# Layer 0 of a four-layer image network: images kept and stored in pairs, one plane kept by halves, one sum moved

## Chip, cores and metric

The kernel runs on one core of one Trainium2 chip. The metric is the device time of one execution in microseconds (us), and the time before is the median of three runs. The core has five engines that run side by side, each taking its instructions strictly in order: PE (TensorE, matrix products), DVE (VectorE), ACT (ScalarE), POOL (GpSimd) and SP (SyncE), which in this kernel issues the transfers between main memory and the on-chip memory.

## What is computed

Four layers, each of the form `x = x + layer(group_norm(x))`, on 32 images of 96 channels and 56 x 56 pixels. The change lies in layer 0, an inverted bottleneck with a gate:

```python
def _L0_conv_ref(x, ...):
    identity = x
    h = jnp.einsum('nchw,oc->nohw', x, w_exp)            # 96 -> 576 channels
    h = jax.nn.silu(_bn(h, g1, b1, m1, v1))
    h = jax.lax.conv_general_dilated(h, w_dw, ...)       # 3x3, each channel by itself
    h = jax.nn.silu(_bn(h, g2, b2, m2, v2))
    s = h.mean(axis=(2, 3))
    s = jax.nn.silu(s @ w_se1.T + b_se1)
    s = jax.nn.sigmoid(s @ w_se2.T + b_se2)
    h = h * s[:, :, None, None]
    h = jnp.einsum('nchw,oc->nohw', h, w_proj)           # 576 -> 96
    h = _bn(h, g3, b3, m3, v3)
    return h + identity

def _gn(v, G=32, eps=1e-5):      # mean and variance over 3 channels x 56 x 56 of one image
...
x = x + _L0_conv_ref(_gn(x), ...)
```

Layer 1 is a wavelet convolution, layer 2 a quantised bottleneck, layer 3 a 9 x 9 convolution of each channel by itself. Between the layers the images lie in main memory as `y`, in which one row of 14 pixels of all 32 images is 32 x 14 x 4 = 1792 bytes: one image has 56 bytes of each such row, a pair of neighbours has 112.

## The kernel before

Layer 0 takes one image after the other, as 96 partitions (channels) by 3136 pixels. The pixels are stored by phase: every fourth column of a tile of 14 rows lies together, so a tile is 4 x 14 rows of 14 pixels. The 576 middle channels are five blocks of 128 partitions: blocks 0 to 2 whole, block 3 whole but convolved in two halves, block 4 with its 64 channels held twice.

One image passes these steps, which the order string `L0_ORDER` (line 59) names by letters. `s` sums the pixels on ACT (`sums`, line 267), `u` sums over the three channels of a group with a small matrix product on PE (`group_sum`), `m` makes the mean on DVE; `q`, `v`, `w` do the same for the squared deviation, and the reciprocal root `rstd` is made on POOL (line 282). `n` normalises on ACT (`xn`, line 295), `r` adds the residual's factor in place (line 301). `eki` expands block k for row tile i on PE (line 309) and puts SiLU of it into a padded plane on ACT (line 313). Blocks 0 to 2 are convolved by nine taps: `f` is the first, on ACT (line 321), `t` one of the other eight, on DVE (line 326). Blocks 3 and 4 are convolved on PE with diagonal matrices (`a`, `c`, line 349), and ACT takes the results out (line 332). `g0` to `g4` make the gate and the gated projection weights `wg`, `p` projects on PE (lines 407 to 410), `d` adds to the image on DVE (line 415), `o` stores it.

The order within one engine is exactly that of the string; a letter followed by `-` belongs to the image before, by `+` to the next one. So the loop is a pipeline over three images, and an engine that waits at a letter also holds back everything that stands behind it on this engine. Three banks of PSUM, the memory that PE writes, are shared by expansion, convolution and projection.

`store` (line 420 and on) issues six transfers of image b, 196 KB each (line 425), then `fetch(b + 3)` (line 196) into the buffer of that image, one of three, and then an equal share of the transfers named `aside`, which lay out convolution matrices of later layers in main memory (lines 520 and 547). `fetch` can be issued only when the image's six stores have landed, and it stands in SP's queue among the others.

Ahead of the loop, `tables()` makes filters for the layers 1 and 3: DVE fills the wavelet tables `zt`, POOL makes the diffusion filter (lines 1108 to 1132), SP stores them. These parts are placed by a scheduler; some buffers of the loop lie where the tables were and wait for their stores.

Of the kernel before, what the change touches and what calls it, by code (L numbers as in the profile page):

```python
# [33 lines left out]
PITCH = W + 1  # L34
NPAD = (H + 2) * PITCH + 2
PAIRS = C // 2
# [25 lines left out]
L0_ORDER = """  # L62
    e00 e01 e02 e03 z0- f0 a3- z2- c1- e10 e11 t01 t02 g0- e12 t03 e30 e40 g1- s+ e13 t04 g2- g3-
    e31 e32 t05 e33 g4- t06 t07 u+ f1 m+ t11 p0- p1- q+ t08 d0- v+ w+ p2- t12 e41 d1- p3- d2- t13
    t14 e20 e21 d3- o- b+ t15 e42 t16 e43 e22 e23 f2 a0 t17 t21 a1 n+ t22 t18 t23 t24 t25 t26 t27 r
# [60 lines left out]

def padded(pool, nc, n, dtype, name):

    out = []
    for i in range(n):  # L130
        t = pool.tile([128, NPAD], dtype, tag=f"{name}{i}", name=f"{name}{i}")
        nc.gpsimd.memset(t[:, : PITCH + 1], 0.0)
        nc.gpsimd.memset(t[:, PITCH : PITCH * (H + 2) : PITCH], 0.0)
        nc.gpsimd.memset(t[:, PITCH * (H + 1) :], 0.0)
        out.append(t)
    return out
# [14 lines left out]


def tiles(t):

    return t.rearrange("c (t p r) q -> c t p (r q)", t=NP, p=NPH)

# [7 lines left out]
@with_exitstack  # L164
def layer0(ctx, tc, S, x, w, y0, norm1, tables, aside):


# [22 lines left out]

    xs = {}

    def fetch(b):
        if b < B:
            xs[b] = pool.tile([C, H * NPH, W4], F32, tag="xt", name="xt", bufs=3)
            nc.sync.dma_start(xs[b], x[b])

# [9 lines left out]
    out4 = load("l0_out", [C, 4])  # L207
    fetch(1)
    fetch(2)

# [20 lines left out]

    eye2 = cp.tile([128, HALF], F32, tag="eye2", name="eye2")
    diag = cp.tile([128, 2, 9, HALF], F32, tag="diag", name="diag")
    hpad = padded(cp, nc, 4, F32, "hpad")
    mv_all = cp.tile([C, B, 2], F32, tag="mv0", name="mv0")
    h2s = [cp.tile([128, H, W], F32, tag=f"h2{i}", name=f"h2{i}") for i in range(2)]


    tables()
    nc.vector.tensor_tensor(eye2, S.ident[:, :HALF], S.ident[:, HALF:], ALU.add)  # L240
# [3 lines left out]
    late = ctx.enter_context(tc.tile_pool(name="l0l", bufs=1))  # L244
    h2s += [late.tile([128, H, W], F32, tag=f"h2{i}", name=f"h2{i}") for i in (2, 3)]
    hab = late.tile([128, NP, 2, NT], F32, tag="hab", name="hab")
    wg = late.tile([128, ND + 1, C], F32, tag="wg", name="wg")
    h2s.append(late.tile([128, H, W], F32, tag="h24", name="h24"))
    hc = late.tile([128, 2, 2, NT], F32, tag="hc", name="hc")

    ims = {}

    def image(b):

        if b not in ims:
            ims[b] = {
                "b": b, "xt": xs.pop(b), "h2": [None] * DV, "ps": [None] * NP,
                "pad": [hpad[(DV * b + k) % 2] for k in range(DV)] + hpad[2:],
                "ss": sm.tile([128, ND], F32, tag="ss", name="ss"),
            }  # L260
        return ims[b]


    def sums(im, name, func, bias):
        im[name] = sm.tile([C, 1], F32, tag=name, name=name)
        junk = pool.tile([C, HW], BF16, tag="junk", name="junk", bufs=1)
        nc.scalar.activation(junk, im["xt"].rearrange("c r q -> c (r q)"), func, bias=bias,
                             accum_out=im[name])

    def group_sum(im, name):  # L270
        im["ps" + name] = psm.tile([C, 1], F32, tag="sm", name="pn")
        nc.tensor.matmul(im["ps" + name], S.grp, im[name], start=True, stop=True)

    def mean(im):
        im["nm"] = sm.tile([C, 1], F32, tag="nm", name="nm")
        nc.vector.tensor_scalar(im["nm"], im["pss1"], -1.0 / HW, None, ALU.mult)

    def deviation(im):
        ve = sm.tile([C, 1], F32, tag="ve", name="ve")
        nc.vector.tensor_scalar(ve, im["pss2"], 1.0 / HW, EPS_GN, ALU.mult, ALU.add)  # L280
        im["rstd"] = sm.tile([C, 1], F32, tag="rstd", name="rstd")
        nc.gpsimd.tensor_tensor(im["rstd"], ve, S.mhalf[:C, :1], ALU.pow)
# [9 lines left out]
    def normalise(im):  # L292
        im["xn"] = pool.tile([C, 2, H, W2], F32, tag="xn", name="xn", bufs=1)
        for p in range(NPH):
            nc.scalar.activation(
                im["xn"][:, p % 2].rearrange("c (t r) (q m) -> c m t (r q)", t=NP, m=2)[:, p // 2],
                tiles(im["xt"])[:, :, p], AF.Identity, bias=im["nb"], scale=im["rstd"])
# [5 lines left out]
    def expand(im, k, i):  # L303

        c = COL[k]
        rows = slice(2 * i * RT, 2 * (i + 1) * RT)
        ps = psum.tile([128, 2, 512], F32, tag="mm", name="ps")
        for j in range(2):
            nc.tensor.matmul(  # L309
                ps[:, j, :NT], wexp[:, k * 128 : k * 128 + 128],  # L310
                im["xn"][:, j, rows, :].rearrange("c h w -> c (h w)"), start=True, stop=True,
            )
        nc.scalar.activation(  # L313
            window(im["pad"][k], 128, 0, 0, 2 * i * RT, 2 * RT).rearrange("p r (w j) -> p j r w", j=2),
            ps[:, :, :NT].rearrange("p j (r w) -> p j r w", w=W2),
            AF.Silu, bias=bi[0][:, c : c + 1], scale=sc[0][:, c : c + 1],
        )

# [16 lines left out]
    def end_block(im, k):  # L335
        silu2(k, im["h2"][k], im["h2"][k], im["ss"][:, k : k + 1])

    def quarters(k, pad, tiles):


        ps = psum.tile([128, 2, 512], F32, tag="mm", name="psd")
        for t in range(9):
            for j in range(2):
                for r in range(2):
                    c = r ^ j
                    p = slice(r * HALF, (r + 1) * HALF)
                    at = (2 * tiles[r] * RT + t // 3) * PITCH + t % 3
                    v = pad[p, at : at + 2 * RT * PITCH].rearrange("p (r w) -> p r w", w=PITCH)
                    nc.tensor.matmul(  # L349
                        ps[c * HALF : (c + 1) * HALF, j, :NT].rearrange("p (r w) -> p r w", w=W2),  # L350
                        diag[p, k - AB, t, :], v[:, :, j:W:2], start=(t == 0), stop=(t == 8),
                    )
        return ps
# [9 lines left out]
    def depthwise_c(im, i):  # L363

        if i == 0:
            im["hc"] = hc
            im["pc"] = sm.tile([128, 2], F32, tag="pc", name="pc")
        ps = quarters(CC, im["pad"][CC], (2 * i, 2 * i + 1))
        silu2(5, im["hc"][:, i], ps[:, :, :NT], im["pc"][:, i : i + 1])
# [30 lines left out]
    def project(im, i):  # L400
        wg = im["wg"]
        rows = slice(2 * i * RT, 2 * (i + 1) * RT)
        ps = im["ps"][i] = psum.tile([128, 2, 512], F32, tag="mm", name="psj")
        for j in range(2):
            out = ps[:C, j, :NT]
            for k in range(DV):
                nc.tensor.matmul(out.rearrange("c (r w) -> c r w", w=W2), wg[:, k, :],  # L407
                                 im["h2"][k][:, rows, j::2], start=(k == 0), stop=False)
            nc.tensor.matmul(out, wg[:, 3 + j, :], im["hab"][:, i, j, :], start=False, stop=False)  # L409
            nc.tensor.matmul(out, wg[:, 5 + (i % 2 ^ j), :], im["hc"][:, i // 2, j, :], start=False, stop=True)  # L410

    def add(im, i):
        for j in range(2):
            v = tiles(im["xt"])[:, i, j::2]
            nc.vector.scalar_tensor_tensor(
                v, im["ps"][i][:C, j, :NT].rearrange("c (x m) -> c m x", m=2), sc3, v, ALU.mult, ALU.add)
        if im["b"] == B - 1:
            store_tile(nc, y0, im, i)

    def store(im):  # L420
        b, xt = im["b"], im["xt"]
        channel_stats(nc, sm, xt, mv_all[:, b, :], "t")
        if b < B - 1:
            for to, of in groups(xt, y0, lambda y: y[:, :, b, :], store=True):
                nc.sync.dma_start(to, of)  # L425
        fetch(b + 3)
        if b < B - 4:
# [452 lines left out]
def layer2(ctx, tc, S, k2, y1, y2, norm3):  # L880
# [187 lines left out]
    def store(im):  # L1068
        b = im["b"]
        channel_stats(nc, sm, im["xt"], mv_all[:, b, :], "t")  # L1070
        if b == B - 2:
            for to, of in groups(im["xt"], y2, lambda y: y[:, :, b, :], store=True):
                nc.sync.dma_start(to, of)
        elif b % 2 and b < B - 1:
            for to, of in groups(im["pair"], y2, lambda y: y[:, :, b - 1 : b + 1, :], store=True):
                nc.sync.dma_start(to, of)
            fetch(b + 5)
# [291 lines left out]
```

## Time and profile before

| | |
|---|---|
| median of 3 runs | 6499.85 us (6497.44 to 6500.72) |
| profiled execution | 6501.16 us |
| its span, first to last instruction | 6499.3 us |
| mean granted TensorE clock | 0.964 of full speed |
| PE busy in the span | 6025.5 us (93%) |
| DVE busy | 5168.3 us (80%) |
| ACT busy | 3953.6 us (61%) |
| POOL busy | 234.1 us (4%) |
| layer 0's last addition | at 3339.9 us |

Times inside the profile are counted from the first instruction. A busy share is a mean over stages with different limits, so what matters for a change in layer 0 is read from the first half of the trace: the waits, the order of time on each engine, and the same stretch of the loop in different images. A matrix product of 32-bit numbers is two instructions in the trace.

### The profile page before, as it was taken

What the parts mean: (1) busy time and instruction counts of PE and PEld (TensorE: products, weight loads), DVE (VectorE), ACT (ScalarE), POOL (GpSimd) and SP (SyncE); (2) the same over time, 40 slices, a digit from 0 to 9 for tenths busy, and PEclk for the clock granted to TensorE, in tenths of its full rate; (3) what the DMA queues carried; (4) which work ended last, traced back from release to release, by engine and by line L of the source; (5) the groups of instructions that cost most, each with busy time, mean ns of one, the idle gap of its engine ahead of it and who ended that gap; (6) DMA issues with size and microseconds to landing.
All of it is one profiled execution on the core that took longest, in us unless ns stands there. A gap on an engine that the chain in (4) does not pass through costs nothing.

```text
span 6499.3 us, 115397 instructions
## 1 busy us (share of the span) xinstructions
PE 6025.5 (93%) x49064; PEld 3599.1 (55%) x49064; DVE 5168.3 (80%) x5469; ACT 3953.6 (61%) x5268; POOL 234.1 (4%) x157
## 2 busy tenths in 40 slices
PE   6989989998998998989969999989999999999699
PEld 3444444444444444444535666667777777778344
DVE  8989979898998998989957766657777767676587
ACT  6556555655656565556635565557767766677355
POOL 4000000000000000000000000000000000000000
PEclk8999999999999999989979999999999999999899
DMA  2486475839539439474655776656869695953888
GB/s 80 29 41 50 41 43 41 46 44 40 47 41 41 43 47 42 39 41 39 17 60 143 141 155 150 143 36 45 48 42 50 44 49 41 51 38 31 166 253 248
DMA packets 1631554, 452.94 MB, mean 70 GB/s; under 512 B 1447406, under 2 KB 1625318, under 8 KB 1627582
## 3 DMA queue, kind: packets, MB, share of 16 engines
q1 hardware_dynamic: 1631038, 445.55, 65.7%
q8 instruction: 386, 6.32, 0.6%
q14 instruction: 130, 1.06, 0.1%
HBM read 284.44 MB, written 214.08 MB: 77 GB/s over the span
## 4 chain that ended last, share of the span: by engine, by line
PE 71%; ACT 9%; DMA 9%; SPq 6%; DVE 3%; issue 1%; POOL 1%; ACTq 0%; DVEq 0%
PE psd L349 14%; PE psd L1019 11%; PE ps L309 9%; PE psj L407 8%; PE pc L735 6%; PE ps L1000 5%; SPq L425 4%; DMA y<-xt 4%; PE pc L1175 3%; PE psj L1056 3%; PE psj L409 3%; PE psj L410 2%; ACT hi L972 2%; ACT a L990 2%; DVE h L326 2%; PE pc L719 2%
## 5 line engine op out<-in xcount | busy, mean ns | idle before, releaser
L326 DVE SCALAR_TENSOR_TENSOR h<-hpad,l_wdw,h 128x3136 f32<-128x3136 f32 x768 | 2659.6, 3480 | 28.7 <-ACT h L321 14.9
L349 PE MATMUL psd<-hpad,diag 64*64 64x392 f32 x13824 | 1239.6, 512 | 13.4 <-issue 13.4
L313 ACT ACTIVATE hpad<-ps,o,s 128x784 f32<-128x784 f32 x640 | 684.3, 1081 | 773.3 <-PE ps L309 771.3
L309 PE MATMUL ps<-xn,l_wexp 96*128 96x392 f32 x2560 | 931.6, 516 | 135.6 <-ACT hpad L313 129.1
L1019 PE MATMUL psd<-apad,diag 64*64 64x392 bf16 x20736 | 931.5, 332 | 110.4 <-ACT a L990 57.2
L349 PEld LDWEIGHTS psd<-hpad,diag 64*64 64x64 f32 x13824 | 547.5, 132 | 694.9 <-issue 656.8
L1019 PEld LDWEIGHTS <-diag 64*64 64x64 bf16 x20736 | 695.6, 107 | 342.3 <-issue 164.7
L309 PEld LDWEIGHTS ps<-xn,l_wexp 96*128 96x128 f32 x2560 | 493.4, 197 | 524.2 <-ACT hpad L313 135.3
L565 ACT COPY T<-raw 32x112 f32<-32x112 f32 (+2 forms) x1440 | 462.8, 384 | 308.1 <-DMA raw<-tdiff 223.3
L990 ACT ACTIVATE u<-ps,o,s 128x784 int16<-128x784 f32 x576 | 536.3, 1002 | 162.0 <-PE ps L1000 143.6
L990 ACT ACTIVATE a<-psd,o,s 128x784 int16<-128x784 f32 x448 | 423.7, 999 | 327.7 <-PE psd L1019 327.7
L407 PE MATMUL psj<-h,wg 128*96 128x392 f32 x1536 | 591.4, 520 | 27.9 <-ACT hpad L313 26.4
L1000 PE MATMUL ps<-hi,l_w1q 96*128 96x392 f32 x1280 | 462.4, 361 | 10.0 <-ACT hi L972 9.2
L1175 PE MATMUL pc<-x,T 128*112 128x416 f32 (+1 forms) x1152 | 415.2, 523 | 48.1 <-DMA raw<-tdiff 47.6
L735 PE MATMUL pc<-x,T 128*112 128x416 f32 (+1 forms) x1152 | 445.8, 523 | 0.0
L1000 PE MATMUL ps<-lo,l_w1q 96*128 96x392 f32 x1280 | 438.0, 342 | 0.0
L407 PEld LDWEIGHTS psj<-h,wg 128*96 128x96 f32 x1536 | 249.4, 166 | 289.3 <-issue 258.3
L1175 PEld LDWEIGHTS pc<-x,T 128*112 128x112 f32 x1152 | 204.7, 178 | 258.1 <-issue 240.7
L332 ACT ACTIVATE hab<-psd,o,s 128x392 f32<-128x392 f32 x256 | 170.6, 671 | 263.5 <-PE psd L349 263.5
L332 ACT ACTIVATE h<-h,o,s 128x3136 f32<-128x3136 f32 x96 | 287.9, 2999 | 19.7 <-DVE h L326 19.7
L321 ACT ACTIVATE h<-hpad,l_wdw 128x3136 f32<-128x3136 f32 x96 | 279.1, 2907 | 9.3 <-DMA twav<-zwav 8.3
L735 PEld LDWEIGHTS pc<-x,T 128*112 128x112 f32 x1152 | 190.9, 178 | 143.9 <-issue 143.9
(202 smaller groups left out, 6793.5 us busy)
## 6 DMA issues: line engine op xcount, KB each, us to landing
X<-y SPq DMA_DIRECT2D x192, 392.0 KB
xt<-in_x_dram SPq DMA_DIRECT2D x32, 1176.0 KB
y<-xt SPq DMA_DIRECT2D x192, 196.0 KB
y<-y SPq DMA_DIRECT2D x96, 392.0 KB
xt<-y SPq DMA_DIRECT2D x96, 392.0 KB
out_dram<-y SPq DMA_DIRECT2D x96, 392.0 KB
y<-xt SPq DMA_DIRECT2D x90, 392.0 KB
twav<-zwav SPq DMA_DIRECT2D x768, 36.8 KB
```

The source lines that it names most:

```text
L309: nc.tensor.matmul(ps[:, j, :NT], wexp[:, k * 128 : k * 128 + 128], im["xn"][:, j, rows, :].rearrange("c h w -> c (h w)"), start=True, sto ...
L313: nc.scalar.activation(window(im["pad"][k], 128, 0, 0, 2 * i * RT, 2 * RT).rearrange("p r (w j) -> p j r w", j=2), ps[:, :, :NT].rearrange ...
L326: nc.vector.scalar_tensor_tensor(h2, window(im["pad"][k], 128, t // 3 - 1, t % 3 - 1, 0, H), wdw[:, k, t : t + 1], h2, ALU.mult, ALU.add,)
L332: nc.scalar.activation(view, ps, AF.Silu, bias=bi[1][:, c : c + 1], scale=sc[1][:, c : c + 1], accum_out=accum)
L349: nc.tensor.matmul(ps[c * HALF : (c + 1) * HALF, j, :NT].rearrange("p (r w) -> p r w", w=W2), diag[p, k - AB, t, :], v[:, :, j:W:2], start ...
L407: nc.tensor.matmul(out.rearrange("c (r w) -> c r w", w=W2), wg[:, k, :], im["h2"][k][:, rows, j::2], start=(k == 0), stop=False)
L565: nc.scalar.copy(to.rearrange("x t (p s) -> x t p s", p=NPH), v[:, k])
L735: nc.tensor.matmul(ps[:PH, to], st["T"][j][:, h, k, :], st["x"][:, j, h, of], start=False, stop=(n == NK - 1))
L990: nc.scalar.activation(out, ps, AF.Identity, bias=o[:, c : c + 1], scale=s[:, c : c + 1])
L1000: nc.tensor.matmul(ps[:, j, :NT], w1[:, k * 128 : k * 128 + 128], im[part][:, r0 : r0 + RT, :].rearrange("c h w -> c (h w)"), start=(part ...
L1019: nc.tensor.matmul(ps[q, j, :NT].rearrange("p (r w) -> p r w", w=W), diag[p, k, t, :], v, start=(t == 0), stop=(t == 8))
L1175: nc.tensor.matmul(ps[:, :, to], st["T"][:, h, k, :], st["x"][:, h, :, of], start=(n == 0), stop=(n == NK - 1))
```

## The change

- An input transfer brings two images, laid out side by side row by row, into one of two pair buffers; the second buffer lies in the pool that comes after the tables. The result of two images is stored together, at the odd one: six transfers of 392 KB, by the function that layer 2 used already. The last two images are stored as before.
- Block 4's plane no longer holds all 56 rows twice: partitions 0 to 63 hold the upper 28 rows, 64 to 127 the lower 28, each with one further row from the other half. Two of its four expansions per image get a second, small ACT instruction for that row.
- The matrix products of convolution and projection read columns as neighbouring pairs instead of every second one, and the projection writes PSUM so that each phase lies together. The addition then reads PSUM in order.
- Each of the two pixel sums is taken in four tiles with four partial sums; the group product has four columns, and a DVE reduction (`total`) stands ahead of the mean and of the deviation.
- In the order, `s+` moves from before `e13` to behind `t07`, ahead of `f1`; `u+` and `m+` move behind `p0-`.
- The unit matrix `eye2` lies in `wg` now, so the diagonal matrices are made after the tables' buffers are free.

```diff
-    e00 e01 e02 e03 z0- f0 a3- z2- c1- e10 e11 t01 t02 g0- e12 t03 e30 e40 g1- s+ e13 t04 g2- g3-
-    e31 e32 t05 e33 g4- t06 t07 u+ f1 m+ t11 p0- p1- q+ t08 d0- v+ w+ p2- t12 e41 d1- p3- d2- t13
+    e00 e01 e02 e03 z0- f0 a3- z2- c1- e10 e11 t01 t02 g0- e12 t03 e30 e40 g1- e13 t04 g2- g3-
+    e31 e32 t05 e33 g4- t06 t07 s+ f1 t11 p0- u+ m+ p1- q+ t08 d0- v+ w+ p2- t12 e41 d1- p3- d2- t13
...
+def store_images(nc, y, im):
+
+    b = im["b"]
+    if b == B - 2:
+        t, at = im["xt"], b
+    elif b % 2 and b < B - 1:
+        t, at = im["pair"], slice(b - 1, b + 1)
+    else:
+        return
+    for to, of in groups(t, y, lambda y: y[:, :, at, :], store=True):
+        nc.sync.dma_start(to, of)
...
+    pairs = [cp.tile([C, H * NPH, 2, W4], F32, tag="xt0", name="xt0")]
 
     def fetch(b):
+
         if b < B:
-            xs[b] = pool.tile([C, H * NPH, W4], F32, tag="xt", name="xt", bufs=3)
-            nc.sync.dma_start(xs[b], x[b])
+            pair = pairs[b // 2 % 2]
+            nc.sync.dma_start(pair, x[b // 2])
+            for j in range(2):
+                xs[b + j] = pair, pair[:, :, j, :]
...
-    fetch(1)
-    fetch(2)
...
-    hpad = padded(cp, nc, 4, F32, "hpad")
+    hpad = padded(cp, nc, 3, F32, "hpad") + padded(cp, nc, 1, F32, "hhalf", HH)
...
     tables()
+    late = ctx.enter_context(tc.tile_pool(name="l0l", bufs=1))
...
+    wg = late.tile([128, ND + 1, C], F32, tag="wg", name="wg")
+    eye2 = wg[:, 0, :HALF]
     nc.vector.tensor_tensor(eye2, S.ident[:, :HALF], S.ident[:, HALF:], ALU.add)
...
+    pairs.append(late.tile([C, H * NPH, 2, W4], F32, tag="xt1", name="xt1"))
+    fetch(2)
...
     def sums(im, name, func, bias):
-        im[name] = sm.tile([C, 1], F32, tag=name, name=name)
-        junk = pool.tile([C, HW], BF16, tag="junk", name="junk", bufs=1)
-        nc.scalar.activation(junk, im["xt"].rearrange("c r q -> c (r q)"), func, bias=bias,
-                             accum_out=im[name])
+
+        im[name] = sm.tile([C, NP], F32, tag=name, name=name)
+        for i in range(NP):
+            junk = pool.tile([C, 2 * RT * NPH, W4], BF16, tag="junk", name="junk", bufs=1)
+            nc.scalar.activation(junk, im["xt"][:, i * 2 * RT * NPH : (i + 1) * 2 * RT * NPH], func, bias=bias,
+                                 accum_out=im[name][:, i : i + 1])
...
+    def total(im, name):
+        t = sm.tile([C, 1], F32, tag=f"t{name}", name=f"t{name}")
+        nc.vector.tensor_reduce(t, im["ps" + name], AX.X, ALU.add)
+        return t
...
+        parts = [(slice(128), 2 * i * RT, slice(2 * RT))]
+        if k == CC:
+            lo, up = slice(64), slice(64, 128)
+            parts = [(up if i // 2 else lo, i % 2 * 2 * RT, slice(2 * RT))]
+            parts += [[], [(up, -1, slice(2 * RT - 1, 2 * RT))], [(lo, HH, slice(1))], []][i]
...
+    def phases(v, j):
+
+        return v.rearrange("p r (q j m) -> p j r q m", j=2, m=2)[:, j]
...
-                        diag[p, k - AB, t, :], v[:, :, j:W:2], start=(t == 0), stop=(t == 8),
+                        diag[p, k - AB, t, :], phases(v[:, :, :W], j), start=(t == 0), stop=(t == 8),
...
-            out = ps[:C, j, :NT]
+            out = ps[:C, j, :NT].rearrange("c (m r q) -> c r q m", m=2, q=W4)
...
-                nc.tensor.matmul(out.rearrange("c (r w) -> c r w", w=W2), wg[:, k, :],
-                                 im["h2"][k][:, rows, j::2], start=(k == 0), stop=False)
+                nc.tensor.matmul(out, wg[:, k, :], phases(im["h2"][k][:, rows], j), start=(k == 0), stop=False)
...
-        fetch(b + 3)
+        store_images(nc, y0, im)
+        if b % 2:
+            fetch(b + 3)
```

More of the change, by code (lines that the diff above doesn't have):

```diff
@@ L34 @@
 PITCH = W + 1
-NPAD = (H + 2) * PITCH + 2
 PAIRS = C // 2
@@ L124, in run_steps, with padded @@
                 step[s[0]](image(b), *map(int, s.rstrip("+-")[1:]))
-def padded(pool, nc, n, dtype, name):
+def padded(pool, nc, n, dtype, name, rows=H):
     out = []
     for i in range(n):
-        t = pool.tile([128, NPAD], dtype, tag=f"{name}{i}", name=f"{name}{i}")
+        t = pool.tile([128, (rows + 2) * PITCH + 2], dtype, tag=f"{name}{i}", name=f"{name}{i}")
         nc.gpsimd.memset(t[:, : PITCH + 1], 0.0)
-        nc.gpsimd.memset(t[:, PITCH : PITCH * (H + 2) : PITCH], 0.0)
-        nc.gpsimd.memset(t[:, PITCH * (H + 1) :], 0.0)
+        nc.gpsimd.memset(t[:, PITCH : PITCH * (rows + 2) : PITCH], 0.0)
+        nc.gpsimd.memset(t[:, PITCH * (rows + 1) :], 0.0)
         out.append(t)
@@ L150, in store_tile @@
         nc.sync.dma_start(to, of)
+def store_images(nc, y, im):
[8 more added lines that the diff above has]
+        nc.sync.dma_start(to, of)
 def tiles(t):
-    return t.rearrange("c (t p r) q -> c t p (r q)", t=NP, p=NPH)
+    return t.rearrange("c (t p r) q -> c t p r q", t=NP, p=NPH)
 def window(t, p, dy, dx, r0, rows):
@@ L230, in layer0 @@
     nc.vector.tensor_tensor(bi3, out4[:, 1:2], bi3, ALU.subtract)
-    eye2 = cp.tile([128, HALF], F32, tag="eye2", name="eye2")
     diag = cp.tile([128, 2, 9, HALF], F32, tag="diag", name="diag")
-    hpad = padded(cp, nc, 4, F32, "hpad")
+    hpad = padded(cp, nc, 3, F32, "hpad") + padded(cp, nc, 1, F32, "hhalf", HH)
     mv_all = cp.tile([C, B, 2], F32, tag="mv0", name="mv0")
@@ L239, in layer0 @@
     tables()
+    late = ctx.enter_context(tc.tile_pool(name="l0l", bufs=1))
+    h2s += [late.tile([128, H, W], F32, tag=f"h2{i}", name=f"h2{i}") for i in (2, 3)]
+    hab = late.tile([128, NP, 2, NT], F32, tag="hab", name="hab")
+    wg = late.tile([128, ND + 1, C], F32, tag="wg", name="wg")
+    eye2 = wg[:, 0, :HALF]
     nc.vector.tensor_tensor(eye2, S.ident[:, :HALF], S.ident[:, HALF:], ALU.add)
@@ L243, in layer0 @@
             nc.vector.tensor_scalar(diag[:, k - AB, t, :], eye2, wdw[:, COL[k], t : t + 1], None, ALU.mult)
[L244 to L247, printed above, removed]
     h2s.append(late.tile([128, H, W], F32, tag="h24", name="h24"))
     hc = late.tile([128, 2, 2, NT], F32, tag="hc", name="hc")
+    pairs.append(late.tile([C, H * NPH, 2, W4], F32, tag="xt1", name="xt1"))
+    fetch(2)
     ims = {}
@@ L255, in image @@
         if b not in ims:
+            pair, xt = xs.pop(b)
             ims[b] = {
-                "b": b, "xt": xs.pop(b), "h2": [None] * DV, "ps": [None] * NP,
+                "b": b, "pair": pair, "xt": xt, "h2": [None] * DV, "ps": [None] * NP,
                 "pad": [hpad[(DV * b + k) % 2] for k in range(DV)] + hpad[2:],
@@ L264, in sums @@
     def sums(im, name, func, bias):
-        im[name] = sm.tile([C, 1], F32, tag=name, name=name)
-        junk = pool.tile([C, HW], BF16, tag="junk", name="junk", bufs=1)
-        nc.scalar.activation(junk, im["xt"].rearrange("c r q -> c (r q)"), func, bias=bias,
-                             accum_out=im[name])
-    def group_sum(im, name):
-        im["ps" + name] = psm.tile([C, 1], F32, tag="sm", name="pn")
-        nc.tensor.matmul(im["ps" + name], S.grp, im[name], start=True, stop=True)
+        im[name] = sm.tile([C, NP], F32, tag=name, name=name)
[3 more added lines that the diff above has]
+                                 accum_out=im[name][:, i : i + 1])
+    def group_sum(im, name):
+        ps = psm.tile([C, NP], F32, tag="sm", name="pn")
+        nc.tensor.matmul(ps, S.grp, im[name], start=True, stop=True)
+        im["ps" + name] = ps
+    def total(im, name):
+        t = sm.tile([C, 1], F32, tag=f"t{name}", name=f"t{name}")
+        nc.vector.tensor_reduce(t, im["ps" + name], AX.X, ALU.add)
+        return t
     def mean(im):
         im["nm"] = sm.tile([C, 1], F32, tag="nm", name="nm")
-        nc.vector.tensor_scalar(im["nm"], im["pss1"], -1.0 / HW, None, ALU.mult)
+        nc.vector.tensor_scalar(im["nm"], total(im, "s1"), -1.0 / HW, None, ALU.mult)
     def deviation(im):
         ve = sm.tile([C, 1], F32, tag="ve", name="ve")
-        nc.vector.tensor_scalar(ve, im["pss2"], 1.0 / HW, EPS_GN, ALU.mult, ALU.add)
+        nc.vector.tensor_scalar(ve, total(im, "s2"), 1.0 / HW, EPS_GN, ALU.mult, ALU.add)
         im["rstd"] = sm.tile([C, 1], F32, tag="rstd", name="rstd")
@@ L295, in normalise @@
             nc.scalar.activation(
-                im["xn"][:, p % 2].rearrange("c (t r) (q m) -> c m t (r q)", t=NP, m=2)[:, p // 2],
+                im["xn"][:, p % 2].rearrange("c (t r) (q m) -> c m t r q", t=NP, m=2)[:, p // 2],
                 tiles(im["xt"])[:, :, p], AF.Identity, bias=im["nb"], scale=im["rstd"])
@@ L312, in expand @@
             )
[L313 to L317, printed above, removed]
+        parts = [(slice(128), 2 * i * RT, slice(2 * RT))]
[3 more added lines that the diff above has]
+            parts += [[], [(up, -1, slice(2 * RT - 1, 2 * RT))], [(lo, HH, slice(1))], []][i]
+        for p, r0, rows in parts:
+            n = rows.stop - (rows.start or 0)
+            nc.scalar.activation(
+                window(im["pad"][k][p], p.stop - (p.start or 0), 0, 0, r0, n).rearrange("p r (w j) -> p j r w", j=2),
+                ps[p, :, :NT].rearrange("p j (r w) -> p j r w", w=W2)[:, :, rows],
+                AF.Silu, bias=bi[0][p, c : c + 1], scale=sc[0][p, c : c + 1],
+            )
     def first_tap(im, k):
@@ L349, in quarters @@
                     nc.tensor.matmul(
-                        ps[c * HALF : (c + 1) * HALF, j, :NT].rearrange("p (r w) -> p r w", w=W2),
-                        diag[p, k - AB, t, :], v[:, :, j:W:2], start=(t == 0), stop=(t == 8),
+                        ps[c * HALF : (c + 1) * HALF, j, :NT].rearrange("p (r q m) -> p r q m", q=W4, m=2),
+                        diag[p, k - AB, t, :], phases(v[:, :, :W], j), start=(t == 0), stop=(t == 8),
                     )
@@ L367, in depthwise_c @@
             im["pc"] = sm.tile([128, 2], F32, tag="pc", name="pc")
-        ps = quarters(CC, im["pad"][CC], (2 * i, 2 * i + 1))
+        ps = quarters(CC, im["pad"][CC], (i, i))
         silu2(5, im["hc"][:, i], ps[:, :, :NT], im["pc"][:, i : i + 1])
@@ L404, in project @@
         for j in range(2):
-            out = ps[:C, j, :NT]
+            out = ps[:C, j, :NT].rearrange("c (m r q) -> c r q m", m=2, q=W4)
+            hab, hc = (im[n].rearrange("p i j (r q m) -> p i j r q m", q=W4, m=2) for n in ("hab", "hc"))
             for k in range(DV):
-                nc.tensor.matmul(out.rearrange("c (r w) -> c r w", w=W2), wg[:, k, :],
-                                 im["h2"][k][:, rows, j::2], start=(k == 0), stop=False)
-            nc.tensor.matmul(out, wg[:, 3 + j, :], im["hab"][:, i, j, :], start=False, stop=False)
-            nc.tensor.matmul(out, wg[:, 5 + (i % 2 ^ j), :], im["hc"][:, i // 2, j, :], start=False, stop=True)
+                nc.tensor.matmul(out, wg[:, k, :], phases(im["h2"][k][:, rows], j), start=(k == 0), stop=False)
+            nc.tensor.matmul(out, wg[:, 3 + j, :], hab[:, i, j], start=False, stop=False)
+            nc.tensor.matmul(out, wg[:, 5 + (i // 2 ^ j), :], hc[:, i % 2, j], start=False, stop=True)
     def add(im, i):
         for j in range(2):
-            v = tiles(im["xt"])[:, i, j::2]
+            n = 2 * i + j
+            v = im["xt"][:, 2 * n * 2 * RT : 2 * (n + 1) * 2 * RT, :]
             nc.vector.scalar_tensor_tensor(
-                v, im["ps"][i][:C, j, :NT].rearrange("c (x m) -> c m x", m=2), sc3, v, ALU.mult, ALU.add)
+                v, im["ps"][i][:C, j, :NT].rearrange("c (r q) -> c r q", q=W4), sc3, v, ALU.mult, ALU.add)
         if im["b"] == B - 1:
@@ L420, in store @@
     def store(im):
[L421 to L425, printed above, removed]
-        fetch(b + 3)
+        b = im["b"]
+        channel_stats(nc, sm, im["xt"], mv_all[:, b, :], "t")
+        store_images(nc, y0, im)
+        if b % 2:
+            fetch(b + 3)
         if b < B - 4:
@@ L1070, in store @@
         channel_stats(nc, sm, im["xt"], mv_all[:, b, :], "t")
[L1071 to L1076, printed above, removed]
+        store_images(nc, y2, im)
+        if b % 2:
             fetch(b + 5)
@@ L1354 @@
     nc = _bacc.Bacc("TRN2", target_bir_lowering=False, num_devices=1)
-    x = a["x"].reshape(B, C, NP, 2 * RT, W4, NPH).transpose(0, 1, 2, 5, 3, 4).reshape(B, C, H * NPH, W4)
+    x = a["x"].reshape(B // 2, 2, C, NP, 2 * RT, W4, NPH).transpose(0, 2, 3, 6, 4, 1, 5).reshape(B // 2, C, H * NPH, 2, W4)
     arrays = {"x": np.ascontiguousarray(x), **layouts(a)}
```

## The prediction

> **What bounds the kernel now.** First the waits, over layer 0's loop (who waited for whom, us in total, times, longest):
>
> ```profile
> ACT junk L267 <- DMA xt<-in_x_dram: 138.6, 7, 27.0
> PE ps L309 <- ACT hpad L313: 127.0, 7, 26.0
> ```
>
> Seven times the first sum waits for its image, and PE behind it waits nearly as long, for ACT to empty PSUM. SP's timeline says why (start, duration): a late image, a normal one, and a pair store of layer 2.
>
> ```profile
> 1518.64 53.45 SPq L425 DMA_DIRECT2D y<-xt  x6
> 1592.60 0.32 SPq L196 DMA_DIRECT2D xt<-in_x_dram  x1
> ...
> 1832.76 27.23 SPq L425 DMA_DIRECT2D y<-xt  x6
> 1870.77 0.34 SPq L196 DMA_DIRECT2D xt<-in_x_dram  x1
> ...
> 4408.93 32.10 SPq L1076 DMA_DIRECT2D y<-xt  x6
> ```
>
> Where six stores take over 50 us instead of 27 to 31, the fetch comes at 74 us instead of 38. Windows from store to store give the price (length; PE, PEld, DVE, ACT, POOL busy; clock; DMA):
>
> ```profile
> 1518.64:1639.97 121.33, 98.67 (x622) 48.76 (x621) 92.78 (x52) 62.14 (x62) 3.63 (x1) 0.89 1.33 36
> 1832.76:1929.07 96.31, 94.90 (x622) 47.28 (x621) 92.69 (x52) 62.00 (x62) 3.63 (x1) 1.00 0.35 45
> ```
>
> From the first store (183.01) to that of image 29 (3158.75) there are 29 such windows, 2975.7 us. The seven late ones last 849.2, the other 22 average 96.7. An undisturbed image is bound by PE and nearly as tightly by DVE. Around the sum it looks so, at clock 1.00:
>
> ```profile
> 1891.18 2.80 ACT L267 ACTIVATE junk<-xt 96x3136 bf16<-96x3136 f32 x1
> ...
> 1897.88 2.98 ACT L313 ACTIVATE hpad<-ps,o,s 128x784 f32<-128x784 f32 x3
> 1900.73 2.90 ACT L321 ACTIVATE h<-hpad,l_wdw 128x3136 f32<-128x3136 f32 x1
> ...
> 1899.00 2.31 PE L407 MATMUL psj<-h,wg 128*96 128x392 f32 x6 [1.41 <-ACT hpad L313]
> ...
> 1904.62 0.15 DVE L276 TENSOR_SCALAR nm<-pn 96x1 f32<-96x1 f32 x1
> ...
> 1912.61 0.25 PE L272 MATMUL pn<-s,grp 96*96 96x1 f32 x2
> ```
>
> The sum delays the evictions, so that PE waits 1.41 us before the projection. `f1` ends at 1903.6, one us before DVE wants it; the last line is `v+`.
>
> **Stores and fetch.** The long stores recur (three runs agree within 3.3 us): images 2, 6, 9, 13, 18, 22, 25, 29. With 56 bytes at 56b in rows of 1792, these are exactly the pieces that cross a multiple of 128 with neither part a multiple of 32. A pair's 112 bytes at multiples of 112 never do, and layer 2's pair stores, laid out alike, take 32.1 to 34.0 us to issue. I take 33.5. Landing adds 11 (38 less 27), a double fetch at most 15 (twice the 7.5 from 1592.60 to the sum at 1600.05): 59.5 us after the first store. The two small transfers between add under a us each. The moved sum starts 66 us after that store (1898.8 less 1832.76, below). So **the late images go**: 849.2 less 7 x 96.7 is **-172**. SP loses 96 issues and nothing behind them gets later.
>
> **The moved sum.** The order of the built programs shows on ACT: `e13`, gate, `e31` to `e33`, four sum pieces, `f1`, four pieces of `q+`. Without the sum ahead of it, `e33` (PE done at 1897.3) is evicted by 1898.8, and PE starts projecting at 1897.3. Then the chain:
>
> - A piece of 784: an instruction of 3136 takes 2804 ns, and 0.84 ns per element lies between 392 elements at 671 ns and 784 at 1000 (results of `psd`); that leaves 0.82 us. Each later piece waits for ACT itself (same `junk`); with the accumulator read of 0.19 I estimate 1.02. Four: 4.1, to 1902.9.
> - `f1` 2.9, to 1905.8. DVE, ready at 1904.6, waits 1.2; behind `t11` are `m+`, `t08`, `d0`.
> - `t11` 3.5, then `total` and mean at 0.15 each (a reduction takes 155 ns, L373): 1909.7.
> - `q+` (2909 instead of 2804): 4.5, to 1914.2. PE's `v+` follows at 1914.3; behind it stand `p2`, `e41`, `p3`.
>
> PE has finished `p0` and `p1` (2 x 6.8 us) at 1910.9, so it waits 3.4 us: a new stall, larger than the 1.4 that goes. `v+` comes 1.7 later than at 1912.6, and behind it PE is full until the next projection: an image takes 96.3 + 1.7 = 98.0.
>
> [...] Row first: after a 2.45 us gap twelve instructions took
>
> ```profile
> 116.13 5.91 PE L309 MATMUL ps<-xn,l_wexp 96*128 96x392 f32 x12 [2.45 <-ACT hc L332]
> ```
>
> against 4.22 at 1893.29: 1.7 lost. Gaps of 1.41 mostly cost nothing. [...] I take 1.0: **99.0 per image, +2.3 on 96.7, times 29: +67**.
>
> **The start.** The built order shows POOL's first `rstd` behind the nine `rev` copies instead of ahead of the tables:
>
> ```profile
> 18.53 0.57 POOL L282 TENSOR_TENSOR rstd<-ve,mhalf 96x1 f32<-96x1 f32 x1 [5.40 <-DVE ve L280]
> ...
> 57.05 17.77 POOL L1123 COPY rev<-yy 96x9 f32<-96x9 f32 x9
> ...
> 34.96 3.48 DVE L326 SCALAR_TENSOR_TENSOR h<-hpad,l_wdw,h 128x3136 f32<-128x3136 f32 x1 [0.53 <-ACT h L321]
> ```
>
> POOL's chain from 26.9 to the copies' end at 74.8 stays; it may begin 5 us earlier, because no further images are loaded ahead of its inputs, although the double first load (about 6 us) and eight pieces precede `rstd`. So `rstd` comes at about 70, not 18.5, and everything of image 0 waits. First tap: 70 + 16.4 (18.53 to 34.96) = 86.4. DVE's second table, queued behind the bias that needs `rstd`, takes 7 us; with its store (10), POOL's clearing and copies (15.5) and the filter's store (5.7, 90.3 to 96.0) the room of `eye2` is free at 109. DVE reaches it after six taps at 107.3, makes the diagonals (4.4) around a seventh, and stands at 117 with 7 taps; five more end at 134.4. Before, DVE had 12 taps done and went on at 91.1: **+43**. The second pair (109 plus 15) is there long before its sum.
>
> **Other edits.** Additions, reading PSUM in order and images in runs of 14: layer 2 does the same, 618 ns against 616, statistics 547: nothing. Half plane: two ACT instructions of 56 elements, 0.3 us each (an estimate from 671 at 392), beside evictions that wait 7 us or 0.23 each for PE: nothing; without this cover 0.6. Normalising from rows of 14: 1100 ns kept (its output is unchanged); the bound above is 1786, of layer 2's `hi`, whose output is more scattered. Four times 0.69, less about 1.5 of free PSUM time, would be 1.2 per image. DVE's two reductions are in the chain.
>
> Pair reads and scattered PSUM writes of PE: the trace has no such row. [...] Row: contiguous f32 products of 392 columns go at 329 ns, layer 2's bf16 ones (L1056) at 168. [...] I take nothing, by the f32 row; the reads are bounded by the strided ones of before (345 against 329 ns): from -1 to +1 us per image.
>
> **Sum** against the profiled execution: -172 + 67 + 43 = -62, so 6501.2 becomes 6439. It lies 1.3 us above the median, far inside my error: **6440**.
>
> **Cases.**
>
> - The forecast (0.68): 6390 to 6495. With 98.0 per image 6410, with 99.7 6460; the start gives 10 either way.
> - The new chain is hidden (pieces and waits shorter, PE not stalled): 95.5 per image saves 35 instead of costing 67: 6338. Against it: DVE has only 1 us of room before `t11`. 0.09.
> - PSUM writes slow (other side): from 2.1 us per image, 8% of the projections, the gain is gone; in full about 7220. [...] 0.12.
> - The pair transfer is late, as a long store: fetched at 74, landed at 89, it would hold the sum 23 us per pair; 14 pairs give +320 and 6760. It decides from 71 us after the store, 4.4 us per pair. Against it all of layer 2's pair stores. 0.06.
> - The change doesn't touch the bound: only if the late images stay while start and chain cost, about 6610. 0.05.
>
> A measurement tells about 0.2%, 13 us, from no change. Faster: most of the first case and the second, 0.74; same 0.06; slower 0.20. The range 6375 to 6510 leaves out two in ten.
>
> **What would show it.** ACT no longer waits for `xt<-in_x_dram` in the loop, and pair stores issue in some 33 us. The windows of an image are 98 to 100 us with PE idle some 3 us before `pn`, released by the second sum, and clock dips behind it. The first tap stands near 86, POOL's first `rstd` near 70. `psj` instructions keep 329 to 345 ns. The forecast falls if a window is over 101.1 us, or if `psj` slows by 8%.

## The result

The changed kernel takes 6423.02 us (median of 4 runs, 6418.54 to 6439.13) against 6498.65 before (4 runs); the ratio is 0.9891, with a 95% interval of 0.9871 to 0.9912. The profiled execution took 6420.77 us, its span is 6419.0, the mean granted clock 0.975. The forecast was 6440. Between the two profiled executions lie 80.4 us, of which the forecast had 62. Split at the last additions of images 0, 29 and 31, the spans show where they came from:

| stretch | before | after | difference | forecast |
|---|---|---|---|---|
| start, to image 0's last addition | 182.9 | 214.2 | +31.3 | +43 |
| 29 images, to image 29's last addition | 2975.7 | 2868.2 | -107.5 | -172 + 67 = -105 |
| images 30 and 31 | 182.3 | 180.4 | -1.9 | 0 |
| later layers | 3158.3 | 3156.1 | -2.2 | 0 |

The waits of the changed kernel over layer 0's loop (who waited for whom, us in total, times, longest) name no fetch any more:

```profile
ACT junk L287 <- DVE nm L302: 116.2, 30, 4.1
...
PE pn L292 <- ACT junk L287: 52.3, 30, 2.2
```

In place of ACT's 138.6 us for `xt<-in_x_dram`, ACT now waits for the mean before its squared sum, once per image, which costs nothing by itself; but PE waits for that squared sum, 52.3 us in 30 waits. SP's timeline (start, duration) shows a pair store and the fetch behind it:

```profile
1697.01 33.45 SPq L162 DMA_DIRECT2D y<-xt  x6
1740.85 0.34 SPq L211 DMA_DIRECT2D xt<-in_x_dram  x1
```

All pair stores of the loop take 32.7 to 35.0 us to issue, and the fetch follows 42 to 45 us behind the start of the store. The window from this store to the next holds two images (length; PE, PEld, DVE, ACT, POOL busy; clock; DMA):

```profile
1697.01:1894.94 197.93, 193.60 (x1242) 93.99 (x1241) 186.19 (x107) 130.16 (x152) 7.26 (x2) 0.98 0.23 44
```

An image takes 98.96 us. Against the undisturbed image of before (96.31) PE is idle 2.2 us instead of 1.4 and busy 96.8 instead of 94.9, with nearly the same number of instructions (621 and 622). PE's timeline shows both at one place (idle time before a row in brackets):

```profile
1966.86 0.26 PE L292 MATMUL pn<-s,grp 96*96 96x4 f32 x2
...
1973.14 0.82 PE L449 MATMUL psj<-hc,wg 128*96 128x392 f32 x2
1975.71 0.33 PE L292 MATMUL pn<-s,grp 96*96 96x4 f32 x2 [1.75 <-ACT junk L287]
1975.90 3.26 PE L447 MATMUL psj<-h,wg 128*96 128x392 f32 x6
1978.96 1.51 PE L448 MATMUL psj<-hab,wg 128*96 128x392 f32 x2
1980.27 0.88 PE L449 MATMUL psj<-hc,wg 128*96 128x392 f32 x2
1980.99 2.23 PE L447 MATMUL psj<-h,wg 128*96 128x392 f32 x6
```

The first `pn` is `u+`, the second `v+`. PE stands idle for 1.75 us before `v+`, and the ten instructions behind it take 5.65 us (3.26 + 1.51 + 0.88) instead of some 3.9: for 3.4 us the granted clock is half (0.50 from 1976.97 to 1980.39). The chain that `v+` waits for runs over ACT and DVE:

```profile
1960.84 0.85 ACT L287 ACTIVATE junk<-xt 96x784 bf16<-96x784 f32 x1
...
1964.64 2.90 ACT L355 ACTIVATE h<-hpad,l_wdw 128x3136 f32<-128x3136 f32 x1
...
1967.57 3.48 DVE L360 SCALAR_TENSOR_TENSOR h<-hpad,l_wdw,h 128x3136 f32<-128x3136 f32 x1 [0.75 <-ACT h L355]
1970.97 0.15 DVE L297 TENSOR_REDUCE ts<-pn 96x1 f32<-96x4 f32 x1
1971.15 0.15 DVE L302 TENSOR_SCALAR nm<-ts 96x1 f32<-96x1 f32 x1
...
1971.40 0.95 ACT L287 ACTIVATE junk<-xt,nm 96x784 bf16<-96x784 f32 x1 [3.86 <-DVE nm L302]
```

There are four pieces (3.8 us), `f1`, then the tap `t11` on DVE, and only behind this tap `total` and mean, although `u+` was done at 1967.1. ACT sits idle for 3.86 us meanwhile. That is the row on which the experiments turn.

At the start (timeline of POOL and DVE):

```profile
50.35 1.21 POOL L1158 COPY rev<-yy 96x9 f32<-96x9 f32 x9
51.51 0.58 POOL L308 TENSOR_TENSOR rstd<-ve,mhalf 96x1 f32<-96x1 f32 x1
...
68.31 21.09 DVE L360 SCALAR_TENSOR_TENSOR h<-hpad,l_wdw,h 128x3136 f32<-128x3136 f32 x6 [3.69 <-ACT h L355]
96.46 0.22 DVE L259 TENSOR_TENSOR wg<-ident 128x64 f32<-128x64 f32 x1 [7.06 <-DMA zdiff<-zt]
```

The reciprocal root (`rstd`) of image 0 stands behind POOL's diffusion work, as foreseen, but comes at 51.5, not at 70: the nine copies take 1.21 us, not 17.77. DVE waits 7.06 us at the unit matrix for the filter's store.

### The profile page after: what moved, and what is told of

Its sections match the earlier page's. It is cut to its first block, busy times and chain, and to the rows that moved or that the text cites. A ratio compares the mean times of both kernels' runs of the same rounds, so it can differ in the third digit from the quotient of the medians.

```text
span 6419.0 us, 115759 instructions
## 1 busy us (share of the span) xinstructions
PE 6013.8 (94%) x49064; PEld 3571.1 (56%) x49064; DVE 5173.8 (81%) x5533; ACT 4052.9 (63%) x5716; POOL 223.1 (3%) x157
## 4 chain that ended last, share of the span: by engine, by line
PE 76%; ACT 13%; DVE 5%; DMA 3%; issue 2%; POOL 1%; SPq 1%; ACTq 0%; DVEq 0%; POOLq 0%
PE psd L388 18%; PE psd L1058 11%; PE ps L335 11%; PE ps L1039 6%; PE pc L774 6%; PE pc L1210 5%; PE psj L447 5%; ACT junk L287 4%; DVE h L360 4%; PE psj L1095 3%; ACT hi L1011 2%; ACT hpad L347 2%; PE pc L758 2%; ACT a L1029 2%; PE psj L448 2%
## 5 line engine op out<-in xcount | busy, mean ns | idle before, releaser
L335 PE MATMUL ps<-xn,l_wexp 96*128 96x392 f32 x2560 | 894.5, 501 | 32.6 <-ACT xn L321 31.5
L388 PE MATMUL psd<-hpad,diag 64*64 64x392 f32 x9216 | 831.1, 511 | 0.0
L347 ACT ACTIVATE hpad<-ps,o,s 128x784 f32<-128x784 f32 x512 | 546.6, 1082 | 305.0 <-PE ps L335 301.8
L335 PEld LDWEIGHTS ps<-xn,l_wexp 96*128 96x128 f32 x2560 | 479.4, 191 | 401.7 <-issue 37.3
L447 PE MATMUL psj<-h,wg 128*96 128x392 f32 x1536 | 606.7, 531 | 15.3 <-ACT hpad L347 7.7
L388 PEld LDWEIGHTS psd<-hpad,diag 64*64 64x64 f32 x9216 | 346.9, 131 | 467.9 <-issue 433.3
L388 PE MATMUL psd<-hhalf,diag 64*64 64x392 f32 x4608 | 417.6, 510 | 0.0
L347 ACT ACTIVATE hhalf<-ps,o,s 64x56 f32<-64x56 f32 (+1 forms) x192 | 163.7, 852 | 340.1 <-PE ps L335 338.3
L1210 PEld LDWEIGHTS pc<-x,T 128*112 128x112 f32 x1152 | 204.1, 178 | 252.6 <-issue 234.3
L388 PEld LDWEIGHTS psd<-hhalf,diag 64*64 64x64 f32 x4608 | 182.7, 132 | 222.9 <-issue 222.6
```

The source lines that it names most:

```text
L335: nc.tensor.matmul(ps[:, j, :NT], wexp[:, k * 128 : k * 128 + 128], im["xn"][:, j, rows, :].rearrange("c h w -> c (h w)"), start=True, sto ...
L347: nc.scalar.activation(window(im["pad"][k][p], p.stop - (p.start or 0), 0, 0, r0, n).rearrange("p r (w j) -> p j r w", j=2), ps[p, :, :NT] ...
L388: nc.tensor.matmul(ps[c * HALF : (c + 1) * HALF, j, :NT].rearrange("p (r q m) -> p r q m", q=W4, m=2), diag[p, k - AB, t, :], phases(v[:, ...
L447: nc.tensor.matmul(out, wg[:, k, :], phases(im["h2"][k][:, rows], j), start=(k == 0), stop=False)
L1210: nc.tensor.matmul(ps[:, :, to], st["T"][:, h, k, :], st["x"][:, h, :, of], start=(n == 0), stop=(n == NK - 1))
```

## The experiments

**Do the long stores come from where the bytes lie?** In the kernel before, seven pairs of neighbours exchange their places in `y`; the later layers take these images exchanged.

```diff
-            for to, of in groups(xt, y0, lambda y: y[:, :, b, :], store=True):
+            n = b ^ 1 if b // 2 in (1, 3, 9, 11) else b + (b in (9, 13, 25)) - (b in (10, 14, 26))
+            for to, of in groups(xt, y0, lambda y: y[:, :, n, :], store=True):
```

> The kernel before, with the stores of seven pairs of neighbours exchanged in y (2 and 3, 6 and 7, 9 and 10, 13 and 14, 18 and 19, 22 and 23, 25 and 26), so later layers take those images in exchanged places. If the long stores come from where the 56 bytes lie (pieces that cross a multiple of 128 with neither part a multiple of 32), they follow the place: images 3, 7, 10, 14, 19, 23 and 26 take 50 to 57 us to issue and 2, 6, 9, 13, 18, 22 and 25 take 27 to 31; the time stays within 10 us of 6499. If they come from something that happens in the same image whatever its place, images 2, 6, 9 and so on stay long.

SP's timeline, the stores of images 2 and 3:

```profile
377.12 29.22 SPq L426 DMA_DIRECT2D y<-xt  x6
...
475.22 57.77 SPq L426 DMA_DIRECT2D y<-xt  x6
```

Now it is image 3, in place 2, whose store is long, and likewise 7, 10, 14, 19, 23 and 26 (50.7 to 58.1 us); images 2, 6, 9 and so on take 27 to 33. One run took 6493.63 us. So the place in `y` makes a store long. That the dividing line is a multiple of 128 fits every image that is stored whole, but another rule that picks the same places would too.

**What of the gain comes with the new order alone?** The kernel before, with only the order string of the change: single images, whole sums.

```diff
-    ... g1- s+ e13 t04 ... t06 t07 u+ f1 m+ t11 p0- p1- q+ ...
+    ... g1- e13 t04 ... t06 t07 s+ f1 t11 p0- u+ m+ p1- q+ ...
```

> The kernel before with the new order alone: single images, whole sums. Late images: the fetch at 74 us lands at 81.5, the sum is wanted at 66 instead of 58, so a late image still loses about 15 us instead of 25: 111 us, seven of them -72. Other images: a whole sum and a whole squared sum make the chain 2.5 us shorter than by pieces, PE's wait at the second group product vanishes, and the wait before the projection goes too: 95.5 us, 22 of them -26. Time about 6400. The rival, that the move itself costs (and not the pieces): ordinary images at 98 to 99, time about 6475.

6399.09 us (2 runs), ratio to before 0.9847 (0.9816 to 0.9877). Waits over the loop, and then windows: an ordinary image, a late one and the one behind it.

```profile
ACT junk L267 <- DMA xt<-in_x_dram: 72.6, 7, 16.4
```

```profile
585.30:680.70 95.40, 94.97 (x622) 46.31 (x621) 92.60 (x52) 62.16 (x62) 3.63 (x1) 1.00 0.40 48
1078.43:1192.57 114.14, 106.42 (x649) 51.36 (x651) 99.97 (x64) 68.13 (x68) 3.63 (x1) 0.97 1.15 39
1192.57:1283.59 91.02, 91.02 (x600) 46.67 (x590) 85.61 (x40) 56.55 (x57) 3.63 (x1) 0.96 0.54 51
```

An ordinary image falls from 96.3 to 95.4 us, PE all but full: the moved sum is a gain where it is one instruction. A late image and the one behind it take 205.2, that is 14.4 over two ordinary ones; over the 29 windows (2872.1 us, less 29 x 95.4, by 7) a late image costs 15.1, where it was 24.6 over the mean of the others. So the rival, that the place of the sum costs, falls, and the wait for the fetch is cut but not gone: for that the pairs are needed. Over the 29 images the order alone gains about as much as the whole change (2872.1 us, and 2868.2 in the changed kernel), and without the late start (182.3 us to image 0's last addition, not 214.2) it is the faster of the two by 24 us.

**Is it the place, with pieces?** The changed kernel with `s+`, `u+` and `m+` in their old places.

```diff
-    ... g1- e13 t04 ... t06 t07 s+ f1 t11 p0- u+ m+ p1- q+ ...
+    ... g1- s+ e13 t04 ... t06 t07 u+ f1 m+ t11 p0- p1- q+ ...
```

> The changed kernel with the first sum, its group product and its mean back in their old places; pairs, halves and sums by pieces stay. If the price of the moved sum is the wait of PE at the second group product and the clock behind it (2.2 us idle and 1.9 us of slower products per image), this order makes the same at another place: four pieces (3.8 us) ahead of the 13th expansion delay its evictions one us more than the single sum of 2.8 did, PE's wait before the projection grows from 1.4 to about 2.4 us, the clock drops there, and an image lasts 98 to 99 us; time 6400 to 6430. The rival, that the place alone costs: 96.3 us per image, about 6345. In either case the pair must have landed 58 us after its store (fetch at 43 to 45 plus about 13); if it is later, ACT waits some us for it in every second image.

6401.53 us (2 runs), ratio to before 0.985 (0.9816 to 0.9884). PE's timeline:

```profile
1855.26 0.25 PE L292 MATMUL pn<-s,grp 96*96 96x4 f32 x2
1857.75 3.30 PE L447 MATMUL psj<-h,wg 128*96 128x392 f32 x6 [2.24 <-ACT hpad L347]
1860.85 1.51 PE L448 MATMUL psj<-hab,wg 128*96 128x392 f32 x2
```

Most images take 98.9 us, as in the changed kernel. The wait is 2.24 us now and stands before the projection, where the kernel before waited 1.41 with one whole sum, and the slow products stand behind it. No wait for a fetch shows: the pair is there in time for the old place too. So in either place the pieces make the chain about long enough to stop PE. The median lies 21 us below the changed kernel's, of which the trace explains 8 (98.64 against 98.90 us per image over 29); two runs of 6392.5 and 6410.6 say no more.

**Is the tap between group product and mean the cost?** The changed kernel with one edit:

```diff
-    ... t06 t07 s+ f1 t11 p0- u+ m+ p1- q+ ...
+    ... t06 t07 s+ f1 p0- u+ m+ t11 p1- q+ ...
```

> The changed kernel with one edit of the order: group product and mean of the first sum ahead of the tap that follows f1, not behind it. The mean then no longer waits for a tap of 3.5 us, the squared sum starts at once behind f1, and the second group product is ready before PE has done its two projections. If PE's wait there, and the low clock behind it, is what the moved sum costs: no wait, PE busy 94.9 instead of 96.8 us per image, an image 95.4 to 95.8 us instead of 98.95, time about 6420 - 29 x 3.4 = 6325. If the clock is low for another cause (the small group products, or activity as such), PE stays at 96.8 us busy, an image at 97 or more, time 6370 or more.

6314.5 us (4 runs), ratio to before 0.9713 (0.9689 to 0.9737): 109 us less than the changed kernel. PE's timeline at `v+`, and two windows of two images:

```profile
1148.71 0.82 PE L449 MATMUL psj<-hc,wg 128*96 128x392 f32 x2
1149.37 0.26 PE L292 MATMUL pn<-s,grp 96*96 96x4 f32 x2
```

```profile
1070.39:1261.17 190.78, 189.93 (x1242) 92.86 (x1241) 186.18 (x107) 130.16 (x152) 7.26 (x2) 1.00 0.24 47
1454.67:1649.18 194.51, 194.51 (x1242) 95.19 (x1241) 186.17 (x107) 130.42 (x152) 7.26 (x2) 0.97 0.23 45
```

`v+` follows at once. Most images take 95.39 us with 94.97 of PE busy: wait and slow products are both gone, as they should be if the one causes the other. The tap alone is not the cost: in the kernel with the new order alone it stands at the same place behind whole sums, and an image takes 95.40. So the tap stops PE only together with the pieces, as far as these two kernels show it (the other one has single images and whole planes too). In the second window the clock falls with no idle time at all; the place is behind the gate's small products:

```profile
1513.82 1.49 PE L425 MATMUL pg<-s1g,l_wse 24*128 24x1 f32 x12
1515.25 5.91 PE L335 MATMUL ps<-xn,l_wexp 96*128 96x392 f32 x12
```

Twelve instructions of the expansion take 5.91 instead of 4.22 us. The clock falls behind these small products in 8 of 31 images; the seven of them after image 0's last addition last 1.1 or 2.6 us longer than 95.4, 13.9 us together, and spread over 29 images this is the difference between 95.4 and the mean of 95.88.

**What made the start late?** First the unit matrix alone, moved to a tap buffer, with the diagonals ahead of the tables:

```diff
-    tables()
...
-    eye2 = wg[:, 0, :HALF]
+    eye2 = h2s[1].rearrange("c h w -> c (h w)")[:, :HALF]
     nc.vector.tensor_tensor(eye2, S.ident[:, :HALF], S.ident[:, HALF:], ALU.add)
...
+    tables()
```

> The changed kernel with the unit matrix in a buffer that is free from the start (the second of the tap buffers) and the 18 diagonal blocks made ahead of the tables. If the late start has two parts, the reciprocal root behind POOL's diffusion work and DVE's stop at the unit matrix until the filter's store has landed, this takes away the second: no wait of 7.1 us at the unit matrix and no 3.0 us of diagonals between the taps; the first tap stays near 68, the twelfth ends near 112 instead of 122.4, image 0's last addition at 204 instead of 214.2, all else as in the changed kernel. A rival, that the late first tap alone sets the start and the taps then wait for something else: the twelfth tap within 3 us of 122.

6403.42 us (2 runs), ratio 0.9849 (0.9827 to 0.9871). The twelfth tap ends at 111.1, image 0's last addition at 206.9. Then image 0's statistics ahead of the tables, and the diffusion work behind them:

```diff
+        for k in "sumqvw":
+            step[k](image(0))
...
+    tables(image(0)["rstd"])
...
-    nc.vector.tensor_scalar(arg, r2, K_EXP2, None, ALU.mult)
+    nc.vector.tensor_scalar(ke, rstd, 0.0, K_EXP2, ALU.mult, ALU.add)
+    nc.vector.tensor_scalar(arg, r2, ke, None, ALU.mult)
```

> The same, and image 0's two sums, mean and deviation stand ahead of the tables, with POOL's diffusion work made to depend on its reciprocal root, so that the root comes first. First tap near 48 instead of 68.3. POOL's nine copies then run beside DVE's taps again, as before the change. If what makes them long is DVE's work at the same time, they take 15 to 20 us instead of 1.2, and the filter's store comes near 90 and lands near 96; if they were long for another reason, 1 to 2 us. The twelfth tap ends at 92 to 98, image 0's last addition at 184 to 190 (214.2 in the changed kernel, 182.9 before).

6391.78 us (2 runs), ratio 0.9831 (0.981 to 0.9852). Timelines of POOL and DVE, first with the early diagonals alone, then with both:

```profile
50.47 1.20 POOL L1158 COPY rev<-yy 96x9 f32<-96x9 f32 x9
51.63 0.58 POOL L308 TENSOR_TENSOR rstd<-ve,mhalf 96x1 f32<-96x1 f32 x1
54.84 2.51 POOL L1167 COPY zt<-rev 96x27 f32<-96x27 f32 x16
...
67.14 28.00 DVE L360 SCALAR_TENSOR_TENSOR h<-hpad,l_wdw,h 128x3136 f32<-128x3136 f32 x8 [7.93 <-ACT h L355]
```

```profile
24.65 0.58 POOL L298 TENSOR_TENSOR rstd<-ve,mhalf 96x1 f32<-96x1 f32 x1 [3.26 <-DVE G L531]
...
48.46 27.99 DVE L350 SCALAR_TENSOR_TENSOR h<-hpad,l_wdw,h 128x3136 f32<-128x3136 f32 x8
...
59.25 17.38 POOL L1166 COPY rev<-yy 96x9 f32<-96x9 f32 x9
...
79.24 9.72 POOL L1175 COPY zt<-rev 96x27 f32<-96x27 f32 x16
```

The same copies take 1.2 us while DVE has no tap running and 17.4 beside its taps; the sixteen others 2.5 and 9.7. Image 0's last addition ends at 185.3, so the two edits take 7.3 and 21.6 of the 31.3 us back.

**Both mended.** The edits of the last three experiments in one kernel:

> Both mended: the early statistics and diagonals, and group product and mean of the first sum ahead of the tap that follows f1. The gains lie in different stretches and should add: about 95.4 to 97 us per image and a start 25 to 30 us earlier than in the changed kernel, 6314.5 - 27 = 6287; 6275 to 6300. If the start is caught up later in the loop, 6305 to 6320.

6285.37 us (5 runs, 6274.55 to 6301.65), ratio to before 0.9672 (0.9653 to 0.9691). Image 0's last addition ends at 184.3, an image takes 95.58 us on average. The gains add, and this version is faster than both kernels.

## Why the prediction was right

**Late images.** Right, and the steps with it: the pair stores were put at 33.5 us and take 32.7 to 35.0, the fetch comes at 42 to 45 (44.5 foreseen), no sum waits for it. The reason, that a pair never lies in the bad places, is shown as far as the exchange of places shows it. The seven late images are worth 172 us of the -107.5; the other 65 are given back in every image.

**The moved sum.** The total was right (99.0 against 98.96 us per image), its two terms were not. The chain was foreseen to end 3.4 us behind PE and ends 1.75 behind. From the start of the projection it is 1.3 us shorter than worked out: the sum starts 0.8 us behind it rather than 1.5, a piece takes 0.98 rather than 1.02, `q+` 4.27 rather than 4.5. The clock, in turn, was put at 1.0 per image, between the 1.7 lost behind a gap of 2.45 us and the nothing lost behind gaps of 1.41, and costs 1.7 in nearly every one. One error covered the other: that 99.0 came out is luck.

How long a wait has to be before the clock falls was the author's estimate; the traces can be counted. The projection behind a wait of 1.41 to 1.43 us ran at full clock in all 13 cases of the kernel before (2.31 us for its first six instructions); behind 1.73 us or more it was slow in 27 of 29 cases of the changed kernel (3.06 to 3.86 us for six, against 2.29 in the other two), and with the sum in its old place, behind 2.23 to 2.37, in 24 of 27. So in this part of the loop 1.75 us can be enough. The records of the granted clock show more: in the traces of the kernel before and of the changed one it changes only on a grid of 3.413 us, to within 0.01 us. Windows of the changed kernel on this grid, two around the wait shown above, then three around one of the two waits that passed:

```profile
1973.56:1976.97 3.41, 1.66 (x7) 0.74 (x6) 3.06 (x6) 2.07 (x4) 0.37 (x1) 1.00 0.17 53
1976.97:1980.39 3.42, 3.42 (x7) 1.51 (x6) 3.42 (x3) 0.00 (x0) 3.26 (x1) 0.50 0.23 72
...
686.74:690.15 3.41, 2.07 (x7) 0.71 (x5) 3.41 (x2) 3.31 (x7) 0.00 (x0) 1.00 0.00 0
690.15:693.56 3.41, 2.60 (x9) 1.38 (x10) 3.06 (x5) 0.76 (x2) 1.72 (x1) 1.00 0.00 0
693.56:696.98 3.42, 3.42 (x11) 1.62 (x10) 2.57 (x3) 0.00 (x0) 1.91 (x1) 1.00 0.00 0
```

In all 27 slow cases the whole wait lies in one stretch of the grid; PE is busy for less than half of that stretch (1.40 to 1.68 us), and the next stretch runs at half clock (0.50). In the two others a line of the grid cuts the wait (here into 1.34 and 0.81 us), and the clock stays full. The two kernels with only the start mended repeat it: of 60 waits of 1.72 to 2.15 us 58 are slow, and the two at full clock are the ones that the grid cuts, laid on by the place of the slow products. Nor are the 27 cases independent: a slow image takes 98.96 us and 29 stretches take 98.99, so the next wait falls at the same place and is slow again. The image of the other cut wait, at 295 us, lasted 97.33 us, so the clock costs about 1.6. With the sum in its old place an image of 98.9 us moves by 0.09 against the grid, and the three cases at full clock come ten or eleven images apart. What share of a stretch is needed is not shown: in that kernel about 1.9 idle us of one stretch passed (an estimate, from the place of the slow products in the other images), in the changed kernel 1.73 did not.

**The start.** The direction was right, the size off by 12 us, and the step is named: "POOL's chain from 26.9 to the copies' end at 74.8 stays". The 17.77 us of the copies were taken from a row in which DVE ran taps beside them; in the same paragraph the first tap was put behind the root, so that no tap runs beside the copies. With 1.2 us, the root comes near 52, the first tap near 68, the unit matrix at 96.5 instead of 109, and +31 is what is left.

**Other edits at nothing.** Right. Away from the low clock, six instructions of the projection with scattered PSUM writes and pair reads take 2.23 to 2.29 us, 2.31 before; `psd` takes 511 ns per instruction, as before; two additions 1.15, as before; normalising 1099 ns. The halo instructions take 401 ns each (0.3 foreseen), beside waits for PE. So scattered PSUM writes and pair reads cost these f32 products nothing here, and the rival "PSUM writes slow" falls; its 7220 was the author's estimate for projections, 27 us per image, of twice the length. Images 30 and 31 and the later layers gain 4 us together, which nothing here explains.

**The rivals.** "The new chain is hidden" was put at 95.5 us per image and 6338. It is not what the change does, but moving `t11` behind `u+` and `m+` in the order makes it so: 95.39 and 6314.5. The late pair transfer falls with the fetches at 42 to 45 us.

## What to carry to other kernels

A stall of an engine is worth what stands behind it: removing 1.75 us of PE's wait gave 3.6 per image, because the clock behind the wait came back too. When a sum is moved in a pipelined order, follow it to its last consumer on every engine; here a tap of 3.5 us between a ready group product and a mean of 0.3 us on the same queue cost nothing behind whole sums (95.40 us per image), the pieces cost nothing without the tap (95.39), and both together cost 3.6. A loss that returns in every round can be one coincidence repeated: compare the length of the round (98.96 us) with the grid on which the clock changes (29 stretches: 98.99). And take a duration from a trace together with the neighbours it was measured beside: the same nine copies took 1.2 us alone and 17.4 beside taps.

## What the hardware showed

- A place in `y` nearly doubled the issue time of a store: 27 to 33 us, or 50 to 58, for the same six transfers of 196 KB in pieces of 56 bytes, by the place alone.
- POOL's small copies took longer beside DVE's taps: nine of them 1.2 us without a tap and 14.1 to 17.8 beside taps, sixteen others 2.5 and 9.7 to 16.8. The memset of `zt` between them took 2.61 or 2.62 us either way. What holds the copies up, and not the memset, is not shown.
- Groups of twelve instructions of one column count as busy in the trace (1.49 us), and yet the clock fell behind them (5.91 us or more for the next twelve of the expansion, 4.22 at full clock), in 9 of the images of the kernel before that wait for no fetch; why it falls in some images and not in others is not shown.
